# The end of a two-layer attention kernel: an earlier verdict, a bank left free, and a first area made by two engines

## The chip, the cores and the metric

The kernel runs on one core of a Trainium2 chip. The metric is device time in microseconds (us) of one execution. Three timed runs of the kernel before gave 3216.32, 3219.51 and 3219.83 us; the median is 3219.51. The profile is of a further execution, which took 3214.37 us, with a span of 3212.4 us from its first to its last instruction. Engines are called PE (matrix products), DVE (VectorE), ACT (ScalarE), POOL (GpSimd) and SP (SyncE, here mostly the issuer of DMAs).

## The reference

The input is 4 images of 256 channels by 64 x 64 pixels in float32. Two layers follow each other, each with a group normalisation (32 groups) and a residual:

```python
x = x + _L0_conv_ref(_gn(x), Wq, Wk, Wv, rel_h, rel_w)
x = x + _L1_conv_ref(_gn(x), w_qkv, b_qkv, w_pe, b_pe, w_proj, b_proj)
```

Layer 0 is attention of 8 heads of 32 channels. Queries are a 1x1 convolution, keys and values are 2x2 convolutions of stride 2 (so 4096 queries meet 1024 keys), and a positional term is added to the keys. Layer 1 splits an image into 4 areas of 1024 pixels, each of which attends to itself, adds a 7x7 depthwise convolution of the values, and ends in a 1x1 projection with bias:

```python
attn = softmax(einsum('bihd,bjhd->bhij', q, k) * scale)
out  = einsum('bhij,bjhd->bihd', attn, v)      # per area of 1024 pixels
out  = out + _dwconv7(v_full, w_pe, b_pe)
return _conv1x1(out, w_proj, b_proj)
```

## The kernel before, in words

The work is cut into 128 units: 2 layers x 4 images x 8 chunks of 512 pixels x 2 groups of four heads. Each unit takes 8 steps of 128 keys. In a step, PE makes the scores of four heads (line 264), ACT takes their exponential (line 268), DVE adds up the exponentials (line 852), and PE weights the values (line 275). No maximum is taken out of the exponent.

After the eight steps of a unit, PE sums the exponentials over the keys (`divisors`, line 285), and the result divides the unit. For all units but the last, `divide` sends the divisors through DRAM to take 512 reciprocals in a narrow shape. For the last unit it takes a full 128 x 512 reciprocal on DVE (line 295) and multiplies (line 296).

Since an exponent can overflow without a maximum, every unit leaves sums of its divisors and their reciprocals in the tile `sums`. After all units a **verdict** is computed from it: DVE compares all of `sums` with a limit (`within`, line 896) and takes the least over a partition (`least`, line 898), PE adds that over the partitions (`count`, line 900), and DVE writes `bad`, the number of partitions that failed (line 901). All five engines then load `bad` into a register (line 1455) and branch past a second, general version of the kernel, which is run when `bad` is over zero (line 1458). After the branch the program closes: the engines meet at line 1495.

The order of work is a plan written by hand: `at(g, j, f)` puts `f` at step `j` of unit `g`. Matrix work beside the attention goes as tasks through a queue `side`, taken up in parts by `advance`. Steps of negative number are a prologue, emitted first. From step 0 on each engine runs its instructions in the written order; `now[0]` is the step, `last` (1024) the first step after the units.

PSUM is shared by tags: `ps_pair` takes one of three pairs of banks (tag `s`), which hold scores and divisors; `side` is one bank for side tasks, and `av` one bank for weighted values. `ps_side` gives a side task the bank `side` while the units run; before step 0 and from `last` on it gives half a pair from `s`.

What comes at the end, in written order, is:

- step 1023: the first half of the product of `project(6, 0)`, the projection of chunk 6, outputs 0 to 127 (bank `side`)
- step 1024: its second half, and its eviction by DVE (line 592)
- step 1025: the divisors of the last unit (a pair of `s`); the convolution added to the first half of chunk 7 (line 577); the first half of the product of `project(6, 1)` (a pair of `s`)
- step 1027: `project_last(7)`, which takes two pairs of `s` for its two outputs. It multiplies half t = 0 of the input for outputs 0 and 1; then DVE divides the last unit, adds the convolution to half t = 1 (line 577) and reduces the divisors and reciprocals into `sums` (line 605, twice); PE multiplies half t = 1; DVE evicts twice (line 613), with a store behind each (line 614). Then come the second half of `project(6, 1)`, its eviction (line 592) and its store (line 595)
- then the verdict.

A matrix product of the projections is written by `product` as four matmuls of 32 columns (line 158); in the profile each is recorded twice, so half a projection has 8 records.

At the beginning, image 0 is loaded, its statistics are taken on DVE (line 342) and turned into a scale and a shift (`norms`, the last step on POOL at line 237). `make_taps` then normalises image 0 area by area, as 8 pieces of 128 x 256 per area by ACT (`normalize`, line 246): piece n is channel half n // 4, row parity n // 2 % 2, and pixel half n % 2. The first products of PE, the keys of layer 0 (`make_k`, tile k0ps), take pieces 0 and 1 first. While these run, DVE's next written work is the statistics of image 1 (tile xs).

Of the kernel before, what the change touches and what calls it, by code (L numbers as in the profile page):

```python
# [9 lines left out]
FP = mybir.dt.float32  # L10
I32 = mybir.dt.int32
AF = mybir.ActivationFunctionType
ALU = mybir.AluOpType
AX = mybir.AxisListType

P = 128
# [30 lines left out]
LIMIT = 1e25  # L47
# [8 lines left out]
def direct_path(  # L56
# [19 lines left out]
    V, S, G, T = nc.vector, nc.scalar, nc.gpsimd, nc.tensor  # L76

    const = ctx.enter_context(tc.tile_pool(name="const", bufs=1))
    pool = ctx.enter_context(tc.tile_pool(name="work", bufs=1))
# [67 lines left out]
    ones = const.tile([P, HD], FP, name="ones")  # L147
# [4 lines left out]
    sums = const.tile([P, 2, len(BLOCKS) * UNITS], FP, name="sums")  # L152

    def product(out, lhsT, rhs, start, stop):

        for i in range(4):
            cols = slice(HD * i, HD * i + HD)
            T.matmul(out[cols, :], lhsT=lhsT[:, cols], rhs=rhs, start=start, stop=stop)  # L158

    def ps_pair(name):  # L160
        return psum.tile([P, 2, CH], FP, tag="s", name=name, bufs=3)

    def ps_side(name):
        if not 0 <= now[0] < last:
            return ps_pair(name)[:, 0, :]
        return psum.tile([P, CH], FP, tag="side", name=name, bufs=1)

# [10 lines left out]
    now, last = [-1], len(BLOCKS) * UNITS * NKT  # L178
# [62 lines left out]
        at(g, j + 1, means)  # L241
        at(g, j + 3, variances)

    def normalize(key, dst, src, t):
        shift, rstd = norms[key]
        S.activation(dst, src, AF.Identity, bias=shift[:, t : t + 1], scale=rstd[:, t : t + 1])  # L246


# [41 lines left out]
    def divide(g, unit):  # L290

        if g == len(units) - 1:

            rb = pool.tile([P, CH], FP, tag="p", name="rb", bufs=10)
            V.reciprocal(rb, dens[g])  # L295
            V.tensor_mul(unit[4]()[:, unit[0], :], avs.pop(g), rb)  # L296
            spare.extend((dens.pop(g), rb))
            return
        den_sb = pool.tile([P, CH], FP, tag="den", name="den_sb", bufs=1)
        few = pool.tile([P, 2, CH // HD], FP, tag="few", name="few", bufs=2)  # L300
        rows = dram.tile([4, CH], FP, tag="rows", name=f"rows_{g}", bufs=4)
        S.copy(den_sb, dens.pop(g))  # L302
        G.dma_start(rows, den_sb[0:P:HD, :])  # L303
        G.dma_start(few[:, 0, :], rows.rearrange("h (q n) -> (h q) n", n=CH // HD))  # L304
        made = {}

        def reciprocals():
            rb = made["rb"] = pool.tile([P, CH], FP, tag="rb", name="rb", bufs=1)
            recs = dram.tile([4, CH], FP, tag="recs", name=f"recs_{g}", bufs=4)
            V.reciprocal(few[:, 1, :], few[:, 0, :])  # L310
            V.tensor_reduce(sums[:, :, g], few, AX.X, ALU.add)  # L311
            G.dma_start(recs.rearrange("h (q n) -> (h q) n", n=CH // HD), few[:, 1, :])  # L312
            for h in range(4):
                G.dma_start(rb[HD * h : HD * h + HD, :], recs[h : h + 1, :].to_broadcast([HD, CH]))  # L314

        def multiply():
            V.tensor_mul(unit[4]()[:, unit[0], :], avs.pop(g), made["rb"])  # L317

        at(g + 1, 7 if g < len(units) - 2 else 4, reciprocals)
        at(g + 2, 4 if g < len(units) - 2 else 0, multiply)  # L320
# [7 lines left out]
    def plan_a(b, u, prep):  # L328

        key = ("A", b)  # L330
# [18 lines left out]
        def make_taps(a, n):  # L349

            t, i, half = n // 4, n // 2 % 2, n % 2
            if n == 0:
                h = pool.tile([P, CT, TA], FP, tag="h", name=f"taps_{b}_{a}", bufs=3)
                taps[a] = h.rearrange("p t (u w n) -> p t u w n", u=2, w=2)
            normalize(
                key,
                taps[a][:, t, i, :, P * half : P * half + P].rearrange("p w (i j) -> p w i j", j=32),
                areas[a][half].rearrange("p t (i u j w) -> p t u w i j", u=2, w=2, j=32)[:, t, i], t,
            )
            if n == 7:  # L360
                areas.pop(a)
# [42 lines left out]
        for a in range(NAREA):  # L404
            g = prep + (2 + 3.1 * a if b else 6 + 2.2 * a)
            at(0, int(NKT * (g - 1.6)), lambda a=a: load(a))
            for n in range(8):
                at(0, int(NKT * (g - 1.1)) + n, lambda a=a, n=n: make_taps(a, n))
            for n in range(2):
                at(0, int(NKT * (g + 0.6 * n)), lambda a=a, n=n: task(4, make_k, a, n))  # L410
                at(0, int(NKT * (g + 0.6 * n + 1.2)), lambda a=a, n=n: task(4, make_v, a, n))
# [6 lines left out]
        def norm_chunk(c, t):  # L418
            normalize(key, hqs[c][:, t, :], hqs[c][:, t, :], t)
# [28 lines left out]
        for c in range(NCH):  # L448
            g = u + 2 * c
# [20 lines left out]
    def plan_b(b, u):  # L470
        key = ("B", b)
# [7 lines left out]
        def norm(a, t):  # L479
            normalize(key, hs[a][:, t, :], hs[a][:, t, :], t)  # L480
# [54 lines left out]
        for a in range(NAREA):  # L535
            g = u + 4 * a
# [31 lines left out]
        def by_column(a):  # L568
            return a.rearrange("p (f q) -> p q f", f=TX)

        def add_conv(c, ts=range(CT)):
            cv, att = rest[c], atts["B", b, c]
            if c < NCH - 1:
                load_residual(c)
            for t in ts:

                V.scalar_tensor_tensor(  # L577
                    by_column(cv[:, t, :]), by_column(cv[:, t, :]), bpe_sb[:, t : t + 1],
                    att[:, t, :].rearrange("p (q f) -> p q f", f=TX), ALU.add, ALU.add,
                )  # L580
# [16 lines left out]
        def project_last(c):  # L597

            cv, xm, ps = rest[c], made_x[c], [ps_pair("ops")[:, 0, :] for _ in range(CT)]
            for t in range(CT):  # L600
                if t == CT - 1:
                    divide(len(units) - 1, units[-1])
                    add_conv(c, [t])
                    for n in range(2):
                        V.tensor_reduce(sums[:, n, len(units) - 1 :], spare[n], AX.X, ALU.add)  # L605
                for to in range(CT):
                    product(
                        ps[to], lhsT=wp_sb[:, t, to * P : (to + 1) * P], rhs=cv[:, t, :],
                        start=(t == 0), stop=(t == CT - 1),
                    )  # L610
            for to in range(CT):
                x_to = xm[:, to, :].rearrange("p (q f) -> p q f", f=TX)
                V.scalar_tensor_tensor(x_to, by_column(ps[to]), bproj_sb[:, to : to + 1], x_to, ALU.add, ALU.add)
                nc.sync.dma_start(ov[b][:, to, c * CH : (c + 1) * CH], xm[:, to, :])

        for c in range(NCH):
            g, j = u + 2 * c + 3, 5
            if b == B - 1 and c == NCH - 1:
                at(g - 2, 2, lambda c=c: load_rest(c))
                at(g - 1, 1, lambda c=c: add_conv(c, [0]))  # L620
                at(g - 1, 3, lambda c=c: project_last(c))
                continue
            at(g - 1, 5, lambda c=c: load_rest(c))
            at(g, j, lambda c=c: add_conv(c))
            at(g, j + 2, lambda c=c: soon_tasks([(2, project, c, to) for to in range(CT)]))
# [186 lines left out]
    units = []  # L812
    for i, (layer, b) in enumerate(BLOCKS):
        u = i * UNITS
        if layer == "A":
            units += plan_a(b, u, u - UNITS)
            plan_norm(("B", b), u + UNITS + 1, 7)
        else:
            units += plan_b(b, u)
# [39 lines left out]
    while now[0] < last or plan or later or side:  # L859
        g, j = divmod(now[0], NKT)  # L860
        if now[0] < last:
            if j == 0:
                ps = {}
# [26 lines left out]
            sum_up(g, j, ps)  # L890
            before = units[g], j, ps[j], av
        now[0] += 1


    within = pool.tile([P, 2 * len(units)], FP, tag="p", name="within", bufs=10)
    V.tensor_scalar(within, sums.rearrange("p k g -> p (k g)"), LIMIT, None, ALU.is_le)  # L896
    least = pool.tile([P, 1], FP, tag="least", name="least", bufs=1)
    V.tensor_reduce(least, within, AX.X, ALU.min)  # L898
    ps = ps_pair("count")[0:1, 0, 0:1]
    T.matmul(ps, lhsT=least, rhs=ones[:, 0:1], start=True, stop=True)  # L900
    V.tensor_scalar(bad, ps, -1.0, float(P), ALU.mult, ALU.add)  # L901


class PairUnit:


# [543 lines left out]
def two_attention_layers(tc: tile.TileContext, *args: bass.AP):  # L1450
    nc = tc.nc
    with tc.tile_pool(name="verdict", bufs=1) as pool:
        bad = pool.tile([1, 1], I32, name="bad")
        direct_path(tc, *args, bad)
        count = nc.values_load(
            bad, min_val=0, max_val=P, skip_runtime_bounds_check_because="a count of partitions"
        )
        with tc.If(count > 0):
            general_path(tc, *args)
# [39 lines left out]
```

## Time and profile before

| what | us |
|---|---|
| median of three runs | 3219.51 |
| the profiled execution | 3214.37 |
| its span | 3212.4 |
| PE busy | 3161.1 |
| ACT busy | 2523.5 |
| DVE busy | 2505.4 |
| POOL busy | 490.0 |
| first k0ps product starts at | 21.19 |
| `bad` written, from | 3201.49 |

The profile is read as times from the start of the span. "A <- B: total, times, longest" is idle time of A that B ended. A busy PE isn't a PE at its peak: the granted clock of the PE changes, and its mean over the span is 0.996 of full speed. Waits, branches and DMA issues aren't counted as busy, so what happens after the last DVE instruction at 3201.49 us shows only in the answers for single lines.

### The profile page before, as it was taken

The page shows a single profiled execution, that of the slowest core. Times are in us where ns is not written, and L with a number is a line of the kernel's source. Part 1 is how long each engine was busy: PE and PEld are TensorE (multiplying, and loading weights), DVE is VectorE, ACT ScalarE, POOL GpSimd, SP SyncE. Part 2 cuts the span into 40 slices and gives each one's busy share as a digit, 9 for nine tenths or more (in the row PEclk, how much of TensorE's full clock was granted, in tenths as well). Part 3 has the DMA queues.
Part 4 walks back from the last instruction along what each step waited for, and adds up shares of the span by engine and source line. Part 5 has one row for each costly group of instructions (what it writes and reads, how often), then busy time and mean ns, then how long its engine had stood idle before and what let it go on. Part 6 is the DMA issues. An engine that isn't in the chain of part 4 may idle for free. (4 is left out here: it accounts for less than half of the span.)

```text
span 3212.4 us, 75608 instructions
## 1 busy us (share of the span) xinstructions
PE 3161.1 (98%) x30762; PEld 960.6 (30%) x30762; DVE 2505.4 (78%) x2715; ACT 2523.5 (79%) x2992; POOL 490.0 (15%) x923
## 2 busy tenths in 40 slices
PE   7999999999999999999999899999999999999997
PEld 4233323233233332332333222323233333222221
DVE  3787897778887778778777677778788788788887
ACT  3888888887887878888887677877778777788775
POOL 0111121111211111111111111111111111111111
PEclk9999999999999999999999999999999999999998
DMA  5232333444544456677766666666555556423212
GB/s 182 57 90 75 91 99 92 102 116 115 131 119 130 121 149 158 177 177 186 184 181 157 173 163 164 165 174 161 152 159 140 157 150 154 129 69 80 66 48 58
DMA packets 648188, 421.50 MB, mean 131 GB/s; under 512 B 411772, under 2 KB 556636, under 8 KB 647832
## 3 DMA queue, kind: packets, MB, share of 16 engines
q1 hardware_dynamic: 619384, 380.11, 46.1%
q0 software_dynamic: 28448, 36.48, 4.2%
q8 instruction: 244, 4.00, 0.5%
q14 instruction: 112, 0.92, 0.1%
HBM read 318.32 MB, written 98.09 MB: 130 GB/s over the span
## 5 line engine op out<-in xcount | busy, mean ns | idle before, releaser
L852 DVE TENSOR_TENSOR p<-p 128x1024 f32<-128x1024 f32 x1790 | 2108.2, 1219 | 505.4 <-ACT p L268 453.5
L268 ACT ACTIVATE p<-s 128x1024 f32<-128x1024 f32 x2048 | 2016.9, 1027 | 516.4 <-PE s L264 501.3
L264 PE MATMUL s<-q,k_A 32*128 32x512 f32 x4096 | 601.4, 639 | 0.5 <-ACT p L268 0.3
L264 PE MATMUL s<-q,k_B 32*128 32x512 f32 x4096 | 594.8, 641 | 0.3 <-ACT p L268 0.3
L275 PE MATMUL av<-p,v_A 128*32 128x512 f32 x4096 | 549.3, 603 | 0.0
L275 PE MATMUL av<-p,v_B 128*32 128x512 f32 x4096 | 545.6, 603 | 0.0
L314 POOL DMA_DIRECT2D rb<-recs x508 | 252.9, 503 | 453.2 <-DMA recs<-few 371.0
L264 PEld LDWEIGHTS s<-q,k_B 32*128 32x128 f32 x4096 | 165.5, 183 | 385.3 <-issue 295.6
L264 PEld LDWEIGHTS s<-q,k_A 32*128 32x128 f32 x4096 | 172.8, 183 | 329.8 <-issue 253.2
L312 POOL DMA_DIRECT2D recs<-few x127 | 70.3, 554 | 1273.6 <-DVE sums L311 1190.7
L275 PEld LDWEIGHTS av<-p,v_A 128*32 128x32 f32 x4096 | 88.6, 108 | 380.7 <-issue 333.0
L275 PEld LDWEIGHTS av<-p,v_B 128*32 128x32 f32 x4096 | 87.7, 108 | 379.6 <-issue 335.9
L158 PE MATMUL ops<-cv,wp_sb 128*32 128x512 f32 x1024 | 135.9, 610 | 8.6 <-DVE sums L605 4.4
L304 POOL DMA_DIRECT2D few<-rows x127 | 72.6, 572 | 456.9 <-DMA rows<-den_sb 447.9
L285 PE MATMUL den<-p,ones 128*32 128x512 f32 x1032 | 140.0, 604 | 1.2 <-DVE p L852 1.2
L303 POOL DMA_DIRECT2D rows<-den_sb x127 | 74.8, 589 | 413.4 <-ACT den_sb L302 406.3
L158 PE MATMUL k0ps<-taps,wkv 128*32 128x256 f32 x2048 | 128.9, 383 | 3.0 <-ACT taps L246 3.0
L158 PE MATMUL q1ps<-h,wqkv_sb 128*32 128x512 f32 x1024 | 131.4, 592 | 0.0
L158 PE MATMUL vals_ps<-hv,wqkv_sb 128*32 128x512 f32 x1024 | 129.9, 592 | 0.0
L158 PE MATMUL k1ps<-h,wqkv_sb 128*32 128x512 f32 x1024 | 128.7, 592 | 0.2 <-ACT cout L798 0.2
L158 PE MATMUL q0ps<-hq,wq_sb 128*32 128x512 f32 x1024 | 128.2, 592 | 0.0
L158 PE MATMUL v0ps<-wkv,taps 128*32 128x256 f32 x2048 | 126.1, 379 | 0.3 <-ACT v_A L396 0.3
(89 smaller groups left out, 1689.1 us busy)
## 6 DMA issues: line engine op xcount, KB each, us to landing
rows<-vals SPq DMA_DIRECT2D x384, 195.9 KB
rb<-recs POOLq DMA_DIRECT2D x508, 64.0 KB, 3.1
share<-vals SPq DMA_DIRECT2D x128, 195.9 KB
vala<-vout SPq DMA_DIRECT2D x128, 144.0 KB
vals<-vout SPq DMA_DIRECT2D x128, 144.0 KB
vc<-vala SPq DMA_DIRECT2D x64, 288.0 KB
band<-mats SPq DMA_DIRECT2D x96, 176.0 KB
hq<-in_x SPq DMA_DIRECT2D x32, 512.0 KB
```

Source lines behind the costliest of these rows:

```text
L158: T.matmul(out[cols, :], lhsT=lhsT[:, cols], rhs=rhs, start=start, stop=stop)
L264: T.matmul(pairs[h // 2][:, h % 2, :], lhsT=k[rows, unit[0], j * P : (j + 1) * P], rhs=q[rows, :], start=True, stop=True,)
L268: exps = [lambda i=i: S.activation(p[i], pairs[i], AF.Exp, scale=SCALE) for i in range(2)]
L275: T.matmul(av[HD * h : HD * h + HD, :], lhsT=v[:, j, unit[0] * P + HD * h : unit[0] * P + HD * h + HD], rhs=p[h // 2][:, h % 2, :], start= ...
L285: T.matmul(dens[g][HD * h : HD * h + HD, :], lhsT=ones, rhs=p[h // 2][:, h % 2, :], start=(n == 0), stop=(n == len(ps) - 1),)
L303: G.dma_start(rows, den_sb[0:P:HD, :])
L304: G.dma_start(few[:, 0, :], rows.rearrange("h (q n) -> (h q) n", n=CH // HD))
L312: G.dma_start(recs.rearrange("h (q n) -> (h q) n", n=CH // HD), few[:, 1, :])
L314: G.dma_start(rb[HD * h : HD * h + HD, :], recs[h : h + 1, :].to_broadcast([HD, CH]))
L852: soon(1, lambda i=i: V.tensor_add(ps[0][i], ps[0][i], ps[j][i]))
```

## The change

Three things are changed.

1. The verdict's instructions move from after the loop into `project_last`: `within`, `least` and the matmul `count` come after the two reductions into `sums` and after the products of half t = 1, and `bad` is written between the first and the second eviction.
2. `ps_side` gives the bank `side` from `last` on as well. Only the tasks of step 1024 and later are touched, that is `project(6, 1)`.
3. For image 0, area 0, the pieces of pixel half 1 (n = 1, 3, 5, 7) are normalised by DVE with a `tensor_scalar`, the other four still by ACT.

```diff
     def ps_side(name):
-        if not 0 <= now[0] < last:
+        if now[0] < 0:
             return ps_pair(name)[:, 0, :]
         return psum.tile([P, CH], FP, tag="side", name=name, bufs=1)
...
-    def normalize(key, dst, src, t):
+    def normalize(key, dst, src, t, by_vector=False):
         shift, rstd = norms[key]
+        if by_vector:
+            V.tensor_scalar(dst, src, rstd[:, t : t + 1], shift[:, t : t + 1], ALU.mult, ALU.add)
+            return
         S.activation(dst, src, AF.Identity, bias=shift[:, t : t + 1], scale=rstd[:, t : t + 1])
...
                 areas[a][half].rearrange("p t (i u j w) -> p t u w i j", u=2, w=2, j=32)[:, t, i], t,
+                b == 0 and a == 0 and half == 1,
             )
...
                         start=(t == 0), stop=(t == CT - 1),
                     )
+
+            within = pool.tile([P, 2 * len(units)], FP, tag="p", name="within", bufs=10)
+            V.tensor_scalar(within, sums.rearrange("p k g -> p (k g)"), LIMIT, None, ALU.is_le)
+            least = pool.tile([P, 1], FP, tag="least", name="least", bufs=1)
+            V.tensor_reduce(least, within, AX.X, ALU.min)
+            count = ps_pair("count")[0:1, 0, 0:1]
+            T.matmul(count, lhsT=least, rhs=ones[:, 0:1], start=True, stop=True)
             for to in range(CT):
                 x_to = xm[:, to, :].rearrange("p (q f) -> p q f", f=TX)
                 V.scalar_tensor_tensor(x_to, by_column(ps[to]), bproj_sb[:, to : to + 1], x_to, ALU.add, ALU.add)
                 nc.sync.dma_start(ov[b][:, to, c * CH : (c + 1) * CH], xm[:, to, :])
+                if to == 0:
+                    V.tensor_scalar(bad, count, -1.0, float(P), ALU.mult, ALU.add)
...
-    within = pool.tile([P, 2 * len(units)], FP, tag="p", name="within", bufs=10)
-    V.tensor_scalar(within, sums.rearrange("p k g -> p (k g)"), LIMIT, None, ALU.is_le)
-    least = pool.tile([P, 1], FP, tag="least", name="least", bufs=1)
-    V.tensor_reduce(least, within, AX.X, ALU.min)
-    ps = ps_pair("count")[0:1, 0, 0:1]
-    T.matmul(ps, lhsT=least, rhs=ones[:, 0:1], start=True, stop=True)
-    V.tensor_scalar(bad, ps, -1.0, float(P), ALU.mult, ALU.add)
```

## The prediction

> **What bounds the kernel now.** PE is busy for 98% of the span (first part of the page), and between 21.19 and 3188.99 us its waits come to under 20 us in all. The change touches none of that, so it can gain only at both ends. I read the timeline at the start, then timeline and waits of the last 25 us, then the single lines of the close.
>
> The start:
>
> ```profile
> 19.76 0.23 POOL L237 TENSOR_SCALAR norm_A<-norm_A 128x2 f32<-128x2 f32 x1
> 20.02 5.74 ACT L246 ACTIVATE taps<-first,norm_A 128x256 f32<-128x256 f32 x11 [1.43 <-POOL norm_A L237]
> 21.19 8.61 PE L158 MATMUL k0ps<-taps,wkv 128*32 128x256 f32 x128 [2.97 <-ACT taps L246]
> 25.47 5.35 DVE L342 BATCH_NORM_STATS2 st_A<-xs 128x6 f32<-128x512 f32 x8 [7.89 <-DMA xs<-in_x]
> ```
>
> ACT makes pieces 5.74 / 11 = 0.52 us apart, PE starts on the second, and DVE lies idle for 7.89 us.
>
> The end, from the timeline:
>
> ```profile
> 3187.47 3.34 DVE L295 RECIPROCAL rb<-den 128x512 f32<-128x512 f32 x1
> 3191.65 1.12 DVE L577 SCALAR_TENSOR_TENSOR cv<-cv,bpe_sb,att_B 128x512 f32<-128x512 f32 x1
> 3192.61 0.67 DVE L605 TENSOR_REDUCE sums<-den 128x1 f32<-128x512 f32 x1
> 3193.43 6.22 PE L158 MATMUL ops<-cv,wp_sb 128*32 128x512 f32 x32 [4.44 <-DVE sums L605]
> 3197.13 0.75 DVE L613 SCALAR_TENSOR_TENSOR xm<-ops,bproj_sb,xm 128x512 f32<-128x512 f32 x1 [3.26 <-PE ops L158]
> 3199.72 0.75 DVE L592 SCALAR_TENSOR_TENSOR xm<-ops,bproj_sb,xm 128x512 f32<-128x512 f32 x1
> 3200.39 0.28 DVE L896 TENSOR_SCALAR within<-sums 128x256 f32<-128x256 f32 x1
> 3201.49 0.15 DVE L901 TENSOR_SCALAR bad<-count 1x1 int32<-1x1 f32 x1 [0.37 <-PE count L900]
> ```
>
> PE waits 4.44 us for the reduction of `den`, because four half-pairs are wanted (den, `project(6, 1)`, two outputs of the last projection) and `s` has three. So 8 records of half t = 0 are left over and 32 stand behind the wait: 8, then 16 of half t = 1, then 8 of `project(6, 1)`. They run at half clock:
>
> ```profile
> 3188.40:3191.90 3.50, 0.59 (x6) 0.00 (x0) 3.36 (x3) 0.00 (x0) 0.00 (x0) 0.99 0.00 0
> 3191.90:3195.30 3.40, 1.87 (x12) 0.65 (x16) 1.97 (x3) 0.00 (x0) 0.00 (x0) 0.50 0.00 0
> 3195.30:3198.70 3.40, 3.40 (x24) 0.89 (x19) 0.75 (x1) 0.00 (x0) 0.00 (x0) 0.50 0.00 0
> ```
>
> (Windows; PE's busy time stands second, the granted clock third from the end.) In the timeline, 8 records take 1.71 us here and 0.85 us at full clock.
>
> After `bad` ends at 3201.64 the span lasts 10.79 us more. Lines 1455, 1458 and 1495 show why (start of first and last at the end of the numbers):
>
> ```profile
> L1455 POOLq TENSOR_LOAD <-bad x1: 947/947/947, 3201.7 to 3201.7; - x1
> L1458 POOLq COMPARE_BRANCH  x1: 50/50/50, 3202.7 to 3202.7; - x1
> L1458 POOLq EVENT_SEMAPHORE  x4: 17/43/43, 3206.7 to 3206.9; - x4
> L1458 POOLq INC_SWDGE_SEM  x1: 1037/1037/1037, 3207.0 to 3207.0; - x1
> L1495 POOLq DRAIN  x3: 40/107/3500, 3208.1 to 3212.2; - x3
> L1495 POOLq EVENT_SEMAPHORE  x4: 17/17/17, 3211.6 to 3212.3; - x4
> ```
>
> POOL loads `bad` (0.95), branches, resumes 3.9 us later, takes 1.04 and a drain of 3.50, and reaches the meeting at 3211.6. ACT, PE and DVE are there by 3206.9 and SP by 3208.8. POOL did nothing else since 3182.2: its close starts when `bad` does, so `bad` sets the end.
>
> [...]
>
> **The change part by part**, against the profiled 3214.37 us (span 3212.4, 1.9 around it); it is 5.1 below the median, so I apply the difference to the median.
>
> *Bank.* `project(6, 1)` now waits for `side`, which line 592 frees at 3186.56 (start 3185.83, 0.73). Its records stood at 3186.26 to 3188, behind `den`. New start some 3186.7. Behind it on PE is only half t = 0, which waits for line 577 until 3187.64 anyway: cost nothing; without that cover 0.4 us. Both outputs' half t = 0 then run while DVE takes its 3.34 us reciprocal, to about 3189.5. What is late next is `cv` half 1, ready at 3191.65 + 1.12 = 3192.77; PE starts at 3192.87. So 0.56 us earlier, with 24 records in place of 32. PE now idles 3.4 in place of 4.44 us[...].
>
> *Verdict.* It removes `within` to `bad` behind the last eviction. DVE has both reductions done at 3193.87. `within` 0.28, then `least` 0.42 with the 0.03 between them: 3194.5. PE's `count` follows 0.15 later at the earliest, and behind the 16 records:
> - full clock: half t = 1 is done for output 0 at 3193.9, for output 1 at 3194.75; `count` ends about 3194.85; DVE is free for the first eviction at 3194.5, done 3195.2; `bad` ends 3195.35.
> - half clock: output 0 done at 3194.8 (0.85 + 1.06 after the start), output 1 at 3196.5; first eviction 3194.85 to 3195.6; `count` about 3196.55; `bad` ends 3196.75.
>
> So `bad` is 6.3 or 4.9 us earlier than 3201.64. Hidden: `within` and `least` (0.7 us) stand ahead of the first eviction on DVE, covered by PE's first product except for 0.5 us at full clock. `count` stands ahead of `project(6, 1)`'s 8 records: some 0.2. `bad` stands ahead of the second eviction: it waits for the same product to within 0.1, costs 0.15. Does anything replace POOL? `project(6, 1)` ends at 3195.8 or 3198.1, its eviction at 3196.7 or 3198.8; DVE then needs 5.2 us (its own 3201.68 to 3206.87 now), arriving at 3201.9 or 3204.0. PE is earlier still. SP issues the last store 0.4 after the eviction; it landed 2.0 after its issue (3202.9), so 3199.2 or 3201.2; SP's last semaphores follow POOL's 1.04 us. POOL needs 10.0 us from `bad`: 3205.3 or 3206.7. POOL stays last by 2.7 us or more, and the closing stays 10.79. No DMA is added; three stores are issued earlier, and SP loads `bad` behind them.
>
> *First area.* PE's first matmul needs pieces 0 and 1. ACT's first ends at 20.02 + 0.62 = 20.64, DVE's starts with it. The trace has no DVE piece of this shape; nearest is `within`, 128x256, 0.28 us, though of contiguous reads. [...] Upper bound 0.75, the line 613 shape with twice the elements. [...] up to 0.6 it is behind ACT's piece, at 0.75 it costs 0.15. PE starts at 20.68, 0.51 earlier. It consumes a pair of pieces in 1.7 us at half clock (ACT supplies one each 0.52), so it isn't starved. If the clock still goes full at 24.3, as it did, half of this counts: 0.26; if the clock moves along, 0.51. I take 0.4. Taking 4 x 0.52 = 2.1 us off ACT gains nothing more, PE having no further wait there.
>
> *Sum:* 0.4 + the mean of 6.3 and 4.9, 5.6, = 6.0. The profiled run has nearly the worst clock at its end (24 of 32 records at half)[...]. So 5.4: 3219.51 - 5.4 = 3214.1, I say 3214.0. That is 0.17%. A measurement of this kernel can tell about 0.2%, 6.4 us, from no change.
>
> **Rivals.**
> 1. *The close isn't tied to `bad`.* POOL's drain of 3.50 us may end on something else, such as the last store (8.7 us before it) or a later engine. For: at the start of the span a drain of POOL takes 0.17, so 3.5 has an unseen cause. Against: no semaphore wait is recorded on it. The stores land 1.7 to 3.7 earlier; with 0.4 the gain is 3.1: 3216.4.
> 2. *The close shrinks as well.* If the drain, run earlier and beside DMAs, takes 0.2, SP or DVE decides: POOL's 1.04 ends 6.4 after `bad`, SP takes 0.8, the end another 0.8. Span end 3203.4 to 3204.8, gain 8.3 with the start: 3211.2.
> 3. *Slower: DVE's pieces queue behind image 1's statistics.* The prologue's order is set by a planner. Should DVE's pieces come behind the sixteen `bn_stats` on xs (25.47 to 38.5), PE starts at about 39.3, 18 later, less 5.5: 3232. It decides once PE starts after 33.1 (21.2 + 5.5 + 6.4), with the sixth chunk ahead. Against: the pieces are written long before, and DVE ran image 0's deviations before those statistics.
> 4. *PE's wait only moves.* It does move, to `cv`; were the verdict still behind the last eviction, the bank would give 0.56 and 8 records, 1.4 to 2.3 us. `count` waiting for `den`'s pair changes nothing: reductions end before `least`.
>
> **Numbers.** Forecast (gain 4.4 to 6.9) 0.58; rival 1 0.20; rival 2 0.14; rival 3 0.05; the rest 0.03, no visible gain. Own range of the forecast: 3212.6 to 3215.1, plus 1.5 for the median of a few runs (their spread is 3.5). For 8 in 10 I take rivals 1 and 2 in: 3210 to 3218. Faster by over 0.2% needs 6.4 us: about a third of the forecast (0.19), most of rival 2 (0.12), a little of rival 1 (0.02): 0.33. Slower: 0.05. Same: 0.62.
>
> **What would show it.** PE's wait ahead of the last projection ends on line 577, with 24 records and `count` behind; `bad` starts before the second eviction, near 3195 to 3197 on the old scale; POOL still closes 10 us after it. [...] k0ps starts 0.5 us earlier. The prediction is wrong if POOL's drain changes, if another engine arrives last at the meeting, or if the start moves later.

## The result and the profile after

The changed kernel took 3210.88 us (median of 12 runs, 3208.33 to 3215.39) against 3216.74 us of the kernel before on the same chip (12 runs, 3215.23 to 3219.83). The ratio is 0.9982, with a 95% interval of 0.9974 to 0.999: 5.9 us faster, a little under what I had called visible. The profiled execution took 3210.07 us with a span of 3208.2 us, 4.2 us less than the span before.

Where these 4.2 us come from is best read against a mark that all kernels here share, the start of the last reciprocal (line 295 before, 298 after): up to it lie the start and the middle, behind it the end.

| us | before | after |
|---|---|---|
| first k0ps product | 21.19 | 20.65 |
| first v0ps product | 29.63 | 29.82 |
| last reciprocal starts | 3187.47 | 3188.07 |
| from there to PE's half t = 1 or what is left ahead of it | 5.96 | 5.32 |
| from there to the end of the last eviction | 13.00 | 10.36 |
| from there to the end of `bad` | 14.17 | 8.88 |
| from the end of `bad` to the last instruction | 10.74 | 11.16 |
| from the last reciprocal to the last instruction | 24.91 | 20.04 |

So the end gave 4.9 us, and start and middle together took 0.6 back. The timeline of the changed kernel's end (start, length, engine and line, operation; in brackets the idle time ahead of it and who ended it):

```profile
3188.07 3.32 DVE L298 RECIPROCAL rb<-den 128x512 f32<-128x512 f32 x1
3192.22 1.12 DVE L581 SCALAR_TENSOR_TENSOR cv<-cv,bpe_sb,att_B 128x512 f32<-128x512 f32 x1
3193.39 3.30 PE L158 MATMUL ops<-cv,wp_sb 128*32 128x512 f32 x16 [2.97 <-DVE cv L581]
3194.81 0.42 DVE L619 TENSOR_REDUCE least<-within 128x1 f32<-128x256 f32 x1
3195.39 0.75 DVE L624 SCALAR_TENSOR_TENSOR xm<-ops,bproj_sb,xm 128x512 f32<-128x512 f32 x1 [0.17 <-PE ops L158]
3196.81 0.14 DVE L627 TENSOR_SCALAR bad<-count 1x1 int32<-1x1 f32 x1 [0.66 <-PE count L621]
3197.68 0.75 DVE L596 SCALAR_TENSOR_TENSOR xm<-ops,bproj_sb,xm 128x512 f32<-128x512 f32 x1
```

PE's wait now ends on line 581, the convolution added to half t = 1; 16 records stand between it and `count`, not 32 as before, and `bad` is written ahead of the last two evictions. The windows of the last products (clock third from the end) show that half clock is still there, for part of the time:

```profile
3190.40:3193.80 3.40, 0.43 (x6) 0.20 (x8) 3.26 (x5) 0.00 (x0) 0.00 (x0) 0.85 0.00 0
3193.80:3197.20 3.40, 3.40 (x26) 0.69 (x18) 2.50 (x7) 0.00 (x0) 0.00 (x0) 0.65 0.05 20
```

POOL's close, by lines 1457, 1460 and 1497 (durations as minimum, median, maximum in ns; then the first and last start):

```profile
L1457 POOLq TENSOR_LOAD <-bad x1: 764/764/764, 3197.0 to 3197.0; - x1
L1460 POOLq EVENT_SEMAPHORE  x4: 17/43/43, 3202.4 to 3202.7; - x4
L1497 POOLq DRAIN  x3: 40/107/3500, 3203.8 to 3207.9; - x3
```

It is the same sequence, its load 4.7 us earlier, its resumption (3202.4) and its drain of 3.50 us 4.3 us earlier. POOL is again the last at the meeting. The start:

```profile
19.98 5.23 ACT L249 ACTIVATE taps<-first,norm_A 128x256 f32<-128x256 f32 x10 [1.43 <-POOL norm_A L237]
19.98 1.38 DVE L247 TENSOR_SCALAR taps<-first,norm_A 128x256 f32<-128x256 f32 x4 [2.44 <-POOL norm_A L237]
20.65 9.35 PE L158 MATMUL k0ps<-taps,wkv 128*32 128x256 f32 x128 [2.46 <-ACT taps L249]
29.82 2.55 PE L158 MATMUL v0ps<-wkv,taps 128*32 128x256 f32 x44
```

PE starts 0.54 us earlier, but its 128 records take 9.35 us in place of 8.61, and the next product starts 0.19 later than before. Up to about 24.3 us before, and about 25.3 us after, PE runs at half speed (here called cold): 8 of its records take 0.85 us and behind that 0.43. This is read from the records alone, since the windows' granted clock says 1.00 there in both kernels. DVE's four pieces took 1.38 us together; one lasts 0.41, and they start 0.32 to 0.33 us apart.

### The profile page after: what moved, and what is told of

Same layout as the page of the kernel before. It is cut to its first block, busy times and chain, and to the rows that moved or that the text cites. A ratio compares the mean times of both kernels' runs of the same rounds, so it can differ in the third digit from the quotient of the medians.

```text
span 3208.2 us, 75608 instructions
## 1 busy us (share of the span) xinstructions
PE 3160.1 (99%) x30762; PEld 960.8 (30%) x30762; DVE 2505.7 (78%) x2719; ACT 2521.8 (79%) x2988; POOL 489.1 (15%) x923
```

## The experiments

My theory: the end is `bad` plus POOL's close, `bad` is set by the records that PE has behind its wait and by PE's clock, and the clock swallows the gain at the start. The main rival: the close hangs on the last store or the last eviction, and the verdict's place is worth nothing. Every run is compared with the kernel before on its own chip. I give the ratio and, from the run's trace, the time from the last reciprocal ("the mark"). Each run has one profile. The diffs are shortened, and what stands behind # in them is a note of mine.

**e1_taps_only**, the third part alone:

```diff
+                b == 0 and a == 0 and half == 1,
```

> Only the third part: DVE makes four of the first area's eight pieces. Theory: k0ps starts 0.5 us earlier (20.65 as in the changed kernel, against 21.19), [...] the shift that reaches the units is anything from -0.2 to +0.5 us, and the time is that of before within 1 us. Rival, the start carries a good part of the 5.9 us: 2 us or more below before.

Ratio 0.9991 (0.9983 to 0.9999), 2.6 us. In the trace nothing of this is seen: k0ps starts at 21.03, 0.67 after the pieces begin (1.17 before), but v0ps at 29.88, and the mark to the end is 24.92 as before (24.91). The pieces began 0.34 us later in this profile; counted from them, v0ps comes after 9.52 us, against 9.61 before. So neither end of the profiled run gained more than 0.1 us. The timed gain is over the 1 us that I expected; its interval, 0.3 to 5.5 us, doesn't exclude that, nor the rival's 2 us, and the trace shows no place for it.

**e2_bank_only**, the second part alone:

```diff
-        if not 0 <= now[0] < last:
+        if now[0] < 0:
```

> Only the second part: project(6, 1) in the bank side, the verdict still behind the last eviction. Theory: PE's wait ahead of half t = 1 ends on the cv line (577) and not on the reduction of den, 24 records in place of 32 behind it, bad starts 1.4 to 2.3 us earlier seen from the start of the last reciprocal, POOL's close stays 10.8 us: 1.4 to 2.3 us below before. Rival, the wait only moves: under 0.6 us.

Ratio 0.9992 (0.9983 to 1.0). Mark to end 22.03, so 2.9 us less than before; `bad` at 11.39 (14.17), close 10.64. From its timeline:

```profile
3201.35 4.08 PE L158 MATMUL ops<-cv,wp_sb 128*32 128x512 f32 x24 [2.96 <-DVE cv L577]
3207.25 0.15 DVE L901 TENSOR_SCALAR bad<-count 1x1 int32<-1x1 f32 x1 [0.37 <-PE count L900]
```

The wait moves to line 577 and 24 records stand behind it. The gain is over the 2.3 us of my upper bound, since the 24 records took 4.08 us: the weight loads among them come 0.43 us apart up to 3202.66 and 0.81 behind that, so the clock fell only a part of the way through. The interval of the ratio reaches 1.0, so the gain stands in the trace and isn't clear of noise in the times.

**e3_verdict_only**, the first part alone (the verdict's instructions moved, `ps_side` as before):

> Only the first part: the verdict in the last projection, project(6, 1) still in a pair of s. Theory (the end is bad plus POOL's close): PE still has 8 + 16 records before count, so bad ends some 2.5 us earlier than before, the last stores no earlier: 2 to 2.6 us below before. Rival (the close hangs on the last store or the last eviction): no gain, perhaps 0.2 us lost.

Ratio 0.9986 (0.998 to 0.9993). Mark to end 20.74, 4.2 us less. This decides between theory and rival: the last eviction is 0.3 us later than before (13.31 against 13.00), the stores with it, and still the end comes 4.2 us sooner. From its timeline:

```profile
3203.75 5.35 PE L158 MATMUL ops<-cv,wp_sb 128*32 128x512 f32 x24 [4.43 <-DVE sums L605]
3209.20 0.15 DVE L622 TENSOR_SCALAR bad<-count 1x1 int32<-1x1 f32 x1 [1.00 <-PE ops L158]
3210.37 0.75 DVE L592 SCALAR_TENSOR_TENSOR xm<-ops,bproj_sb,xm 128x512 f32<-128x512 f32 x1 [0.37 <-PE ops L158]
```

`bad` ends 11.54 after the mark, 2.6 earlier, as worked out. The other 1.5 us I hadn't expected: the close took 9.20 and not 10.74. POOL's load of `bad` took 0.49 (0.95 before, where five engines load at once) and it resumed 2.9 after its branch (4.0 before).

**e4_early_verdict** makes `bad` ahead of the last reciprocal by leaving the last unit out of the verdict (254 of 256 columns):

```diff
+                at(g - 2, 5, lambda: early(0))    # within, least
+                at(g - 1, 1, lambda: early(1))    # count
...
+                at(g - 1, 3, lambda: early(2))    # bad
```

> The changed kernel with a verdict that leaves out the last unit (254 of 256 columns of sums), so that it needs no product of the last projection: within and least at step 1021, count at step 1025, bad ahead of the last reciprocal. Theory: POOL starts its close near the last reciprocal, 8 us earlier, and is no longer last at the meeting; DVE (5.2 us behind line 596's eviction) or SP (last store, then 1.5 us) sets the end, about 3 us below the changed kernel. Rival (the close hangs on the last store): the time of the changed kernel.

Ratio 0.9969 (0.9958 to 0.9981); mark to end 16.06, 4.0 us below the changed kernel. By its line of the meeting:

```profile
L1506 POOLq DRAIN  x3: 40/107/3500, 3197.3 to 3208.4; - x3
L1506 SPq DRAIN  x3: 7/7/13, 3207.8 to 3208.1; - x3
```

POOL's drain starts at 3197.3 and lasts 3.50 us in the middle of the last projection, so it doesn't hang on the last store, nor on the other engines' arrival. SP is now last, held by the last store: it was issued at 3203.02, and SP passed its wait at 3206.7. So in this run an earlier verdict alone brings the end no further than some 16 us behind the mark.

**e5_warm_tail**: the changed kernel with three idle matmuls in PE's pause.

```diff
+                    warm = psum.tile([P, CH], FP, tag="av", name="warm", bufs=1)
+                    for _ in range(3):
+                        T.matmul(warm, lhsT=wp_sb[:, 0, :P], rhs=cv[:, 0, :], start=True, stop=True)
```

> The changed kernel with three idle matmuls of 128 x 128 on 512 columns (0.85 us each at full clock, into the free bank av, read by nobody) between PE's half t = 0 and its wait for line 577. Theory: PE's pause falls under 1 us, the 16 records of half t = 1 run at full clock, bad ends near 7.4 us after the start of the last reciprocal in place of 8.9, and the span's end follows it by the same 1.5 us. Rival, bad isn't held by the clock: no change.

Ratio 0.9977 (0.9967 to 0.9987). From its timeline:

```profile
3195.05 1.92 PE L158 MATMUL ops<-cv,wp_sb 128*32 128x512 f32 x16 [0.20 <-DVE cv L581]
3196.46 0.42 DVE L622 TENSOR_REDUCE least<-within 128x1 f32<-128x256 f32 x1
3197.46 0.13 DVE L630 TENSOR_SCALAR bad<-count 1x1 int32<-1x1 f32 x1
```

The 16 records take 1.92 us in place of 3.30, and `bad` ends 7.89 after the mark, not 8.88. It isn't 7.4 because `least` on DVE now comes last, and then an eviction stands ahead of `bad`. That the end of the kernel follows by as much isn't shown. It came at 18.18, which is 1.9 us less than in the changed kernel's first profile (20.04), but only 0.2 less than in its second (e9: `bad` at 9.16, end at 18.35): the close took 10.29 here, 11.16 and 9.19 there. The ratio can't be told from the changed kernel's either.

In e6 and e7, whose end is that of the changed kernel, the clock held, and `bad` came at 7.87 and 7.89 with no idle matmuls in the pause. So the half clock is worth 1.0 to 1.3 us of `bad` here. The pause is 2.97 us in all four profiles, so its length doesn't tell when the half clock comes. In the granted clock of the profiles before and after, a half clock with PE work in it lasted 3.41 us (before from 1782.15, after from 3192.80) or 6.83, twice that (before from 1833.35 and 3191.85, after from 1834.30). Here is PE's work (its busy time second) in stretches of that length: the one with most of the pause, first in the changed kernel, then in e9, and the two that share the pause in e6:

```profile
3189.39:3192.80 3.41, 1.03 (x10) 0.12 (x2) 3.27 (x3) 0.00 (x0) 0.00 (x0) 1.00 0.00 0
3198.70:3202.11 3.41, 0.44 (x8) 0.11 (x8) 3.27 (x4) 0.00 (x0) 0.00 (x0) 1.00 0.00 0
3189.15:3192.56 3.41, 1.94 (x18) 0.58 (x10) 3.31 (x2) 0.00 (x0) 0.00 (x0) 1.00 0.00 0
3192.57:3195.98 3.41, 1.91 (x16) 0.42 (x16) 3.31 (x7) 0.00 (x0) 0.00 (x0) 1.00 0.00 0
```

Behind stretches with 30% and 13% of PE work the clock fell; behind 57% and 56% it held. In e5 the stretch from 3192.81 to 3196.22 holds 3.21 us of PE work (94%), of which the idle matmuls are all but 1.17 (34%).

**e6_warm_head** and **e7_warm_head_act**: idle matmuls around the statistics products, so that PE's clock is full at the start; e7 gives all pieces back to ACT.

```diff
+            if key == ("A", 0):
+                warm(6)          # ahead of the first product; 2 and 6 behind the two products
```

> The changed kernel with idle matmuls of 128 columns in the prologue (6 ahead of the first statistics product once the last chunk of image 0 has landed, 2 between the two statistics products, 6 behind them), read by nobody. Theory: the clock is full when k0ps starts, its 128 records take 6.8 to 7.2 us in place of 8.4 to 9.2, and the first v0ps product starts 1.3 to 2.3 us earlier than the 29.8 of the changed kernel, at the cost of at most 0.4 us in the start of the statistics products. Rival, the start is held by the pieces from ACT and DVE: v0ps not earlier.

> As the kernel with the warm start, but all eight pieces of the first area by ACT, as before. Theory: with the clock full, PE uses a pair of pieces in 0.85 us and ACT makes one in 1.04, so PE starts 0.5 us later and is then held by the pieces: v0ps starts 0.5 to 1.0 us later than with the pieces on two engines. Rival, the third part is worth nothing: under 0.2 us.

Ratios 0.9977 (0.9969 to 0.9986) and 0.9979 (0.9973 to 0.9986). From the two timelines, e6 first:

```profile
16.96 0.43 PE L230 MATMUL gm_A<-mv_A,gmat 128*128 128x2 f32 x2
21.14 7.11 PE L158 MATMUL k0ps<-taps,wkv 128*32 128x256 f32 x128 [1.02 <-ACT taps L260]
28.07 3.21 PE L158 MATMUL v0ps<-wkv,taps 128*32 128x256 f32 x56
```

```profile
21.70 7.67 PE L158 MATMUL k0ps<-taps,wkv 128*32 128x256 f32 x128 [1.52 <-ACT taps L260]
29.18 1.05 PE L158 MATMUL v0ps<-wkv,taps 128*32 128x256 f32 x16
```

At full clock 128 records take 7.11 us, and v0ps starts 1.75 us earlier than in the changed kernel's first profile (1.19 earlier than in its second, e9), though the first statistics product comes 0.76 later than in the first (16.20), more than the 0.4 that I allowed. Without DVE's help v0ps is 1.11 us later: by these two profiles the third part is worth that much when PE runs at full speed. In the changed kernel the cold start hides most of it. Counted from the first piece, v0ps came after 9.61, 9.93 and 9.91 us in the three cold profiles with ACT alone (before, e2, e3), and after 9.84, 9.52, 9.44, 9.93 and 9.50 in the five with both engines (changed, e1, e4, e5, e9): 0.2 us less in the mean, and the two ranges overlap. In the timed runs e6 and e7 can't be told apart.

**e8_all_earlier**, with nothing left out, joins the warm start, the warm end and an earlier verdict:

```diff
-                        V.tensor_reduce(sums[:, n, len(units) - 1 :], spare[n], AX.X, ALU.add)
+                        S.activation(junk, spare[n], AF.Identity, bias=0.0 if n else rb[:, 0:1],
+                                     accum_out=sums[:, n, len(units) - 1 :])
...
+                    if t == CT - 1 and to == 0:
+                        count = ps_pair("count")[0:1, 0, 0:1]
+                        T.matmul(count, lhsT=least, rhs=ones[:, 0:1], start=True, stop=True)
+            V.tensor_scalar(bad, count, -1.0, float(P), ALU.mult, ALU.add)
```

The bias adds one of the reciprocals to each divisor, so that ACT reads the divisors' bank only after DVE has; a sum that is too large is still found.

> The changed kernel with the warm start, the warm end, and a verdict that is earlier still, with nothing left out: the 254 columns of the earlier units are compared at step 1021, ACT sums the last unit's divisors and reciprocals in place of DVE, and count stands between the products of outputs 0 and 1, bad ahead of the first eviction. Theory: bad ends about 6.7 us after the start of the last reciprocal, POOL still closes 10 us later and the last store's landing is close behind it; from the reciprocal to the end 17.5 us in place of 20.0, and 3.5 to 4.5 us below the changed kernel with the start. Rival, the stores or evictions hold the close now: 19 us or more from the reciprocal.

Ratio 0.9968 (0.9956 to 0.998). `bad` at 6.68, mark to end 15.99, 1.5 us below what I expected, since the close took 9.31. I took its early comparison to stand where DVE is full: PE waited 1.16 us for DVE ahead of den's products, 0.46 in e5.

**e9_changed_again** and **e10_better**: the changed kernel and e8 with two things altered, on one chip. In e10 the early part covers 126 units at step 1018, and 4 idle matmuls stand in place of 6.

> The changed kernel itself, on the chip of the next run, for a direct comparison. Theory: 0.9982 of before as on record, within its interval 0.9974 to 0.999; from the start of the last reciprocal to the end 18.2 to 20.1 us, as the granted clock in the last products falls.

> The kernel e8_all_earlier with two things mended and nothing left out: the early part of the verdict covers the first 126 units and stands at step 1018, where DVE has room, and the idle matmuls ahead of the first statistics product are 4 in place of 6. Theory: the first k0ps product starts 0.3 to 0.5 us earlier and the last reciprocal isn't held back by 0.7 us; 1 us below e8_all_earlier, so 4 to 5.5 us below the changed kernel, ratio to before 0.9955 to 0.997; from the reciprocal to the end 16.0 us. Rival, the ends no longer matter beside the spread of the middle: the ratio of the changed kernel.

The changed kernel: 3215.42 against 3221.85, ratio 0.9979 (0.9973 to 0.9986). e10: 3212.03, ratio 0.997 (0.996 to 0.9981), 3.4 us below the changed kernel; I had said 4 to 5.5. First k0ps product at 20.48 and v0ps at 27.41 (20.43 and 29.26 in e9), mark to end 16.10 (18.35): 1.85 + 2.25 = 4.1 us in the traces. With e8 (ratio 0.9968), from which it can't be told, it is the fastest kernel of this study that leaves nothing out, though its interval overlaps that of the changed kernel. One aim was missed: the wait ahead of den's products is still there, 1.30 us, so the place of the early comparison isn't shown to be its cause. The profile also shows how ACT takes over DVE's sums:

```profile
3185.78 2.52 PE L299 MATMUL den<-p,ones 128*32 128x512 f32 x14 [1.30 <-DVE p L894]
3192.31 0.69 ACT L632 ACTIVATE junk<-den,rb 128x512 f32<-128x512 f32 x1 [8.05 <-DVE rb L309]
3194.29 1.06 PE L158 MATMUL ops<-cv,wp_sb 128*32 128x512 f32 x8 [0.21 <-DVE five L638]
3195.47 0.14 DVE L651 TENSOR_SCALAR bad<-count 1x1 int32<-1x1 f32 x1 [1.01 <-PE count L650]
```

Beside all this stands the middle. In the two profiles of the same changed kernel, the mark is at 3188.07 and at 3196.66 us. PE's waits between 1500 and 1900 us (total, times, longest) are one place where they part, the first profile ahead of e9's:

```profile
PE conv_ps L800 <- DMA share<-vals: 6.4, 2, 4.7
PE conv_ps L800 <- DMA rows<-vals: 1.7, 1, 1.7
PE ops L158 <- DVE xm L596: 1.7, 1, 1.7
```

```profile
PE conv_ps L800 <- DMA share<-vals: 6.8, 2, 5.3
PE ops L158 <- DVE xm L596: 4.7, 1, 4.7
PE conv_ps L800 <- DMA rows<-vals: 2.6, 2, 1.4
```

These add to 9.8 and 14.1 us. That accounts for half of the 8.6; the rest is in smaller pieces that I didn't trace. The three parts alone multiply to a ratio of 0.9969, the whole has 0.9979 to 0.9982; with such a spread the difference means nothing.

## Why the prediction was right

The time fell by 5.9 us where 5.4 was forecast, within the range of 4.4 to 6.9. The end is why: moving the verdict and freeing the bank bring `bad` forward, and POOL's close follows it. The absolute time, 3210.88, lies 1.7 us below the forecast's own range of 3212.6 to 3215.1, since the median before fell from 3219.51 (three runs) to 3216.74 (twelve). That the sum agrees to 0.5 us is in part luck. The step from its 6.0 to 5.4, 0.6 us for the clock at the end of the kernel before, was an estimate of mine that no run shows. The profile gave 4.2 us, the start's 0.4 isn't in it, and the close, taken as fixed, differs by 2.0 us between two profiles of the changed kernel.

- *Bank.* Right. PE resumes 5.32 us after the mark, 5.40 was worked out; `project(6, 1)` starts at 3187.20, right behind the end of the eviction that frees the bank (3187.14), and nobody waited for it. PE's pause was 2.97 us where I had 3.4.
- *Verdict.* Right in mechanism and size. The forecast gave `bad` at 7.88 after the mark with full clock and 9.28 with half; that either could come was my estimate, from the 0.85 and 1.71 us that 8 records took before. The runs of this end had 8.88, 9.16, 7.87 and 7.89: the full clock occurs, and a clock that is half for a part of the time. In my sum `least` ends at 3194.5; the terms add to 3194.6, without consequence.
- *POOL stays last and the close keeps its length.* Right for who is last in the changed kernel. Rival 1 falls by e3, where the end moved with `bad` and not with the stores, and by e4, where POOL's drain was over 2.2 us before the last store was even issued. Rival 2 falls since the drain takes 3.50 us in every profile; what it is spent on, none of them shows. The length of the close wasn't constant: 11.16 in the profile after, 9.19 in e9. The load of `bad` and the resumption after the branch move, and I had taken them as fixed.
- *The last store lands 2.0 after its issue.* Wrong, without consequence. In the changed kernel it was issued at 3198.46, and SP passed its wait at 3203.0, over 4 us later. From 3199.32 to 3201.25, 5 packets of the queues q8 and q14 (of kind "instruction" by the page) ran beside the store's; before, the first of them came at 3203.55, when the stores' last packet had ended (3202.90). SP stayed 2.8 us ahead of POOL. That lead isn't safe. In e7, whose end has the same instructions, SP needed 2.01 us to issue the last store, not 0.38, and reached the meeting 0.3 us behind the end of POOL's drain (3202.1 + 3.50); in e10 SP was 0.1 us behind it. The lines are e7's:

```profile
L1508 POOLq DRAIN  x3: 40/107/3500, 3202.1 to 3206.5; - x3
L1508 SPq DRAIN  x3: 7/7/13, 3205.9 to 3206.2; - x3
```

- *First area.* The start (20.68, measured 20.65) was right: a DVE piece lasts 0.41, below the 0.6 up to which I had counted it as free. The term for its worth, 0.4 us, isn't borne out: v0ps came 0.2 later in this profile, 0.4 earlier in e9 (29.26), and in the cold profiles, counted from the first piece, it comes 0.2 earlier in the mean. I had bounded it between a clock that rises at a fixed time and one that moves along with PE. In this run full speed came a full microsecond later than before (25.3 against 24.3), and in e9, which is the same kernel, at 24.3 again; it neither kept to one time nor followed PE's start. The 1.1 us of e6 against e7 show only with a warm PE. The 2.6 us of e1's timed runs stay unexplained.
- *Rival 3*, pieces queued behind image 1's statistics: didn't occur; DVE's pieces start at 19.98, the statistics at 25.43.

## What to carry to other kernels

Ask what starts the close of a kernel with a branch at its end: here 9.2 to 11.2 us (before, changed, e2, e3, e5, e8, e9) lay between the end of a single number that DVE writes and the last instruction, POOL's drain of 3.50 among them, and in e3 the end came 4.2 us sooner though the last eviction was 0.3 later. It pays until another engine closes later: here SP with the last store, some 16 us behind the mark. Look at a wait for PSUM together with the records that pile up behind it and the clock that they get: before it was 4.44 us, with 32 records behind it that took 6.22, a part of them at a granted clock of 0.50. In e5, with three idle matmuls in a pause that couldn't be avoided, the 16 records behind it took 1.92 us in place of 3.30. Where a profile's middle moves by more than the change is worth (here 8.6 us between two profiles of one kernel, against 5.9), measure from a mark beside the change.

## What the runs showed that I hadn't expected

- Loading one number into a register took 0.86 to 0.98 us in the three kernels where five engines did it at once (before, e1, e2), and 0.46 to 0.50 on ACT, POOL and PE in the runs where those were alone, except once in the changed kernel (0.73 to 0.76).
- POOL resumed 3.9 to 4.1 us after its branch in the three kernels whose engines branch together. Where the branches are spread it took 2.6 to 4.6 us, and in two runs of the same changed kernel 4.6 and 2.9. What sets it, I can't say; it is the largest uncertainty left in the end.
- The DMA packets of the last stores took at most 0.12 to 0.13 us where the branch came behind the stores (before, e1, e2), and up to 0.23 to 0.80 us (0.80 in the changed kernel) where packets of the instruction queues ran beside them (all the others).
- The granted clock fell behind stretches that still held PE work: 1.03 us of 3.41 (30%) at the changed kernel's end, 1.12 (33%) at 1782 us in the kernel before, and as much as 1.66 (49%) at 1643 us in e1. It held behind 1.51 us (44%) at the end of e7. It fell with a pause of PE of 2.97 us (changed kernel, e9) and of 2.71 (at 1782 us before), and held with one of 2.97 in e6 and e7.
